# A GRU layer over 128 steps: state weights loaded over 128 rows, and the state kept in the order that this needs

## The chip, the cores and the metric

The kernel runs on one core of one Trainium2 chip. The time is the device time of one execution in microseconds (us). Engines have short names: PE is TensorE (matmuls; PEld its weight loads), ACT is ScalarE, DVE is VectorE, POOL is GpSimd, SP is SyncE, which here only issues DMAs. Each engine works through its own queue in the order of the program.

## The reference, cut to what matters

A GRU layer with a residual, in float32. x is (64 batch rows, 128 steps, 512 features), the state h is (64, 512), first taken from `cond_1024`:

```
for t in 0..127:
    z = sigmoid([x_t, h] @ Wz + bz)
    r = sigmoid([x_t, h] @ Wr + br)
    c = tanh([x_t, r * h] @ Wh + bh)
    h_new = (1 - z) * h + z * c
    out[:, t] = x_t + h_new
    h = tanh(h_new @ Wp + bp) if t % 4 == 3 and t < 127 else h_new
```

Wz, Wr, Wh are (1024, 512): the upper 512 rows multiply x, the lower 512 the state. Wp is (512, 512).

## The kernel before, in words

**Two kinds of matmul.** The products with x do not depend on the state; groups of four steps are computed ahead of time by two levels of a fast (Strassen-like) scheme, as "filler" units that DVE and POOL combine into sums `cp`. The products with the state are the recurrence. Both go through `products` (line 222), a matmul with a 32-column stationary operand.

**Layout.** The 64 batch rows are cut into two halves of 32 (h = 0, 1), the 512 features into four quarters of 128. A state tile is [128 partitions, 2 halves, 128 columns]: partition 32*q + b holds batch row b of a half and quarter q of the features; the 128 columns are the features of the quarter. To multiply, DVE transposes each half in blocks of 32 x 32 (`turn`, line 251). After it, column block k of 32 holds, on partition 32*q + e, the feature that stood in column 32*k + e of quarter q. The rows of a weight tile must lie in the same order: `load_w` (line 96) puts row 128*q + 32*k + e on partition 32*q + e, place k, which takes one DMA of 32 partitions for each quarter. The x side of the kernel has another order already: `load_wx` (line 116) puts row 4p + k on partition p, place k, and `join_x` (line 258) transposes x while reading it with a step of four elements.

**One step of a half** (`half`, line 836): gate r on PE (4 weight blocks x 2), then `crossed` (line 246): two ACTIVATEs of 64 x 128, one for each pair of quarters, from the gate's PSUM bank to r in PSUM; DVE multiplies r * h (line 853) and turns it into rhT (line 854). Meanwhile PE does gate z and some fillers; then the candidate gate from rhT. After both halves' z gates, `gate_z` (line 870) crosses z for both halves, four ACTIVATEs into PSUM, and DVE makes keep = (z - 1) * h (line 873). `crossed` with tanh writes c to SBUF; DVE forms h_new = c * z - keep (lines 912, 925) and turns it into hT for the next step's r gate. In every fourth step the propagation gate (`wp`, `bias_p`) follows, with its own tanh, turn, and fillers. In the last seven steps, z is crossed a half at a time (`late`, line 686). POOL adds h_new to the residual rows `xr` (line 811), and SP stores these four steps at a time.

`seed` (line 395) has ACT copy the sums of the x products into a gate's PSUM bank ahead of its state products, and `copied` (line 513) has ACT take filler sums out of PSUM.

**Order of the work.** The two halves are generators, interleaved by a count of columns with the second 700 behind (lines 951 to 963). `PLACES` (line 623) says how many filler units a half does at three places of a step (between gate z and the candidate gate; after the candidate; after the propagation gate), with one triple for each of the eight steps of a round; the first number is 1 in four of the eight steps and 6 in the other four. `HEAD` gives the first steps more (up to 16), `TAIL` the last ones fewer. A round starts at step 3, 11, 19 and so on.

**The head.** SP and ACT issue the loads of x and of the x weights; `load_wh` (line 149) then loads the state weights gate by gate, two DMAs by SP and two by ACT for each gate; Wp follows by SP alone in `later_loads`. POOL issues the loads of h0 into `h_init`, from which DVE turns the first hT (line 668).

Of the kernel before, what the change touches and what calls it, by code (L numbers as in the profile page):

```python
# [18 lines left out]
def kernel(  # L19
# [14 lines left out]
    nc = tc.nc  # L34
    B, T, D = x.shape
    H = h0.shape[1]
    P = 128
    S = 2
    V = B // S
    NQ = P // V  # L40
    J = H // NQ
    C = 2
    K = D // P
# [28 lines left out]
    wh = [const.tile([P, K, H], F32, name=f"wh_{i}") for i in range(3)]  # L72
    wp = const.tile([P, K, H], F32, name="wp")

    tw_all = const.tile([P, 3, S * NQ * 3 * J // 2], F32, name="tw")
# [6 lines left out]
    gates_in = (Wr, Wz, Wh)  # L82
# [3 lines left out]
    def part(q):  # L86
        return slice(q * V, (q + 1) * V)
# [5 lines left out]
                    out=tile_[part(q), j : j + n, h, :], in_=x[ts(h, V), t0 : t0 + n, ts(q, J)]  # L93
                )

    def load_w(wt, w, k0=0, k1=K, engs=(nc.sync, nc.sync)):
        for q in (0, 2, 1, 3):
            engs[q // 2].dma_start(
                out=wt[part(q), k0:k1, :],
                in_=w[q * P + k0 * V : q * P + k1 * V, :].rearrange("(k e) n -> e k n", e=V),  # L100
            )

    both_queues = (nc.sync, nc.scalar)

    xr = {}
# [10 lines left out]
    def load_wx(i, k0, k1):  # L116
# [2 lines left out]
            in_=gates_in[i][:D].rearrange("(p k) n -> p k n", k=K)[:, k0:k1],  # L119
        )  # L120

    h_init = two.tile([P, S, J], F32, tag="h", name="h_init")
    bias_x = const.tile([P, C, S, 3, J // 2], F32, name="bias_x")
    bias_p = const.tile([P, S, J], F32, name="bias_p")
# [17 lines left out]
    nc.gpsimd.tensor_copy(held, wx[0:1, 2, R, 0:1])  # L142
    for h in range(S):
        nc.gpsimd.dma_start(
            out=h_init[:, h, :],
            in_=h0[ts(h, V), :].rearrange("b (q j) -> q b j", q=NQ),
        )

    def load_wh(i):
        load_w(wh[i], gates_in[i][D:], engs=both_queues)  # L150

    xs = {}

# [23 lines left out]
    def gate_ps(i, h):  # L177
        return rec[2][:, 0] if i == Z else rec[h][:, 0 if i == R else 1]
# [57 lines left out]
    def product(ps, h, lT, w, k, start=False):  # L236
# [6 lines left out]
            start,  # L243
        )

    def crossed(dst, h, i, func):
        for d in range(2):
            nc.scalar.activation(dst[ts(d, 2 * V)], gate_ps(i, h)[ts(h, 2 * V), d, :], func)  # L248

    def turn(dst, src):  # L250
        nc.vector.transpose(out=dst, in_=src)

    def new_T(tag, name):
        return two.tile([P, S, P], F32, tag=tag, name=name)
# [44 lines left out]
    def sum_outer(n):  # L299
        for ka in range(S):  # L300
            if n == 3:
                nc.gpsimd.tensor_sub(tw[3][:, ka], outer(1, 1, ka), outer(0, 1, ka))
            elif n == 2:
                nc.gpsimd.tensor_add(tw[2][:, ka], tw[3][:, ka], outer(0, 0, ka))
            else:
                nc.gpsimd.tensor_sub(tw[4][:, ka], outer(1, 0, ka), tw[2][:, ka])
# [27 lines left out]
    def sum_raw12(g):  # L334
        v = xT[g]
        sx[g, 12] = one.tile([P, 4, C, B], F32, tag="s12r", name=f"s12r_{g}")
        four([sx[g, 12][:, n] for n in range(4)], v[:, 0], v[:, 1])
# [19 lines left out]
    def sum_s34(g):  # L357
        v = xT[g]
        o = sx[g, "o34"] = one.tile([P, 2, 2, P], F32, tag="o34", name=f"o34_{g}")
        nc.gpsimd.tensor_sub(o[:, 0], v[:, 0:2, 0, :], v[:, 2:4, 0, :])  # L360
        nc.gpsimd.tensor_sub(o[:, 1], v[:, 0:2, 1, :], sx[g, "o12"][:, 1])
        s = sx[g, 73] = one.tile([P, 4, 2, B], F32, tag="s73", name=f"s73_{g}")
        four([s[:, n] for n in range(4)], o[:, :, 0], o[:, :, 1])
# [225 lines left out]
    def outer_1(g):  # L589
        with_bias(g, 1, bias0)  # L590

    def outer_c11(g):
        add(c_block(g, 0, 0), m_(g, 1), m_(g, 2))
# [14 lines left out]
    def outer_c22(g):  # L608
        add(c_block(g, 1, 1), m_(g, 7), m_(g, 5))

    def outer_c21(g):
        add(c_block(g, 1, 0), m_(g, 7), m_(g, 4))

    def pair_left(a, p1, p2, g=1):
        with_bias(g, p2, bias0)
        add(c_block(g, a, 0), m_(g, p1), m_(g, p2))

    def pair_right(a, p1, x_, g=1):
        with_bias(g, x_, bias_x[:, 1])
        add(c_block(g, a, 1), m_(g, p1), m_(g, x_))  # L620
# [44 lines left out]
    join_x(0, 2)  # L665
    hT = new_T("hT", "hT_init")
    for h in range(S):
        turn(hT[:, h, :], h_init[:, h, :])
    for i in (1, 2):
        sum_inner(i, nc.vector, slice(2, 3))  # L670
# [86 lines left out]
    def behind_step(t, duo, u, h_new):  # L757
        g, j = divmod(t, Q4)
        even, odd = FIRST + 2 * duo, FIRST + 2 * duo + 1
        if t == T - 7:  # L760
            pair_left(0, 1, 2, LAST)
            pair_right(0, 1, 10, LAST)
        if t == 0:
            sum_outer(2)
            sum_outer(4)
        if t == 3:
            pair_left(1, 8, 9)
            pair_right(1, 8, 11)

        if duo >= 0:  # L770
            if u == 0 and duo >= 1 and odd - 2 < LAST:
                outer_c22(odd - 2)
                outer_c21(odd - 2)
            if even * Q4 < T:
                if u == 0:
                    sum_s34(even)
                elif u == 1:
                    outer_1(even)
                    outer_c11(even)
                    sum_raw12(odd)  # L780
                elif u == 2:
                    outer_u1(even)
                    outer_5(even)
                    sum_raw4(even)
                elif u == 3:
                    outer_c12(even)
                    outer_u2(even)
                    outer_c22(even)
                    if odd < LAST:
                        sum_s12(odd)  # L790
                elif u == 4:
                    if odd < LAST:
                        sum_s34(odd)
                    outer_c21(even)
                    if odd < LAST:
                        outer_1(odd)
                elif u == 5 and odd < LAST:
                    sum_raw4(odd)
                elif u == 6 and odd < LAST:
                    outer_u1(odd)  # L800
                    outer_c11(odd)
                elif u == 7 and odd < LAST:
                    outer_5(odd)
                    outer_c12(odd)
        if duo >= -1 and (even + 2) * Q4 < T:
            if t == 2 or (u == 6 and duo >= 0):
                sum_raw12(even + 2)
            if u == 7:
                sum_s12(even + 2)
        if t < T - 1:  # L810
            nc.gpsimd.tensor_add(xr[g][:, j], xr[g][:, j], h_new)  # L811

        n = 0
        if t >= T - CHUNK:
            n = 3 if t == T - 2 else 0
        elif j == Q4 - 1:
            n = 4
        if n:
            for h in range(S):
                for q in range(NQ):  # L820
                    nc.sync.dma_start(  # L821
                        out=out[ts(h, V), t - n + 1 : t + 1, ts(q, J)],
                        in_=xr[g][part(q), j - n + 1 : j + 1, h, :],
                    )
        if j == 1 and g >= 1 and (g + 1) * Q4 < T:
            new_xr(g + 1)
            load_x(xr[g + 1], (g + 1) * Q4, Q4)
        if t in (1, 2):
            load_xs(t + 2)
        if duo >= 0:  # L830
            if u == 3:
                load_xs(odd + 2)
            elif u == 7:
                load_xs(even + 4)

    def half(h):

        for t in range(T):
            g, j = divmod(t, Q4)
            prop = j == CHUNK - 1 and t < T - 1  # L840
            last = t == T - 1
            duo, u = divmod(t - 3, 8)
# [22 lines left out]
            keep = new_two("keep", t)  # L865
# [4 lines left out]
            def gate_z(part, halves, h_old=h_old, z_=z_, keep=keep):  # L870
                for i in halves:
                    crossed(z_[:, i, :], i, Z, AF.Sigmoid)
                nc.vector.scalar_tensor_tensor(  # L873
                    out=keep[:, part, :],
                    in0=z_[:, part, :],
                    scalar=1.0,
                    in1=h_old[:, part, :],
                    op0=ALU.subtract,
                    op1=ALU.mult,
                )  # L880
                if last:
                    o = xr[g][:, j, part, :]
                    nc.vector.tensor_sub(o, o, keep[:, part, :])

            if h == 1:
                if late(t):
# [19 lines left out]
            h_new = new_two("h", t)  # L906
# [4 lines left out]
            c = z_[:, h, :]  # L911
            nc.vector.tensor_mul(c, cand[:, h, :], c)  # L912
            if last:
                o = xr[g][:, j, h, :]
                nc.vector.tensor_add(o, c, o)
                if h == 0:
                    nc.sync.dma_start(
                        out=out[ts(h, V), t, :].rearrange("b (q n) -> q b n", q=NQ), in_=o
                    )
                else:  # L920
                    for q in (0, 2, 1, 3):
                        both_queues[q // 2].dma_start(out=out[ts(h, V), t, ts(q, J)], in_=o[part(q)])
                return
# [31 lines left out]
    while any(live):  # L955
        h = 0 if live[0] and (not live[1] or at[0] <= at[1]) else 1
# [46 lines left out]
```

## Time and profile before

| | us |
|---|---|
| median of 3 runs | 1260.61 (1259.17 to 1260.79) |
| the profiled execution | 1259.52 |
| its span in the profile | 1257.6 |
| PE busy | 1250.6 (99%) |
| ACT busy | 837.9 (67%) |
| POOL busy | 891.5 (71%) |
| DVE busy | 805.5 (64%) |

A row of the profile names the line, engine and operation, then "out<-in" by the program's names, the shapes, the number of instructions, their busy time and the mean of one in ns, and the engine's idle time before them with what ended it. A row of the timeline has its start and length in us. "PEld" rows are weight loads; here the stationary operand is the turned state, so a PEld row that reads hT or rhT is where PE takes up what DVE has turned.

### The profile page before, as it was taken

How to read it: one execution, taken by the hardware profiler on the slowest of the kernel's cores; microseconds unless marked ns; L12 is line 12 of the kernel's file. 1: busy time of each engine (PE TensorE's matmuls, PEld its weight loads, DVE VectorE, ACT ScalarE, POOL GpSimd, SP SyncE). 2: the span in 40 equal slices, each digit the busy share in tenths (PEclk: the TensorE clock that was granted, in tenths of full speed). 3: DMA queues.
4: the chain of work that ended last, by engine and by line, in shares of the span. 5: the costliest groups of instructions: out<-in, count | busy, mean ns of one | idle time of the engine just before them, and what ended most of it. 6: DMA issues, size and time to landing. Idle time of an engine off the chain costs nothing.

```text
span 1257.6 us, 60730 instructions
## 1 busy us (share of the span) xinstructions
PE 1250.6 (99%) x25960; PEld 1162.1 (92%) x25960; DVE 805.5 (64%) x2173; ACT 837.9 (67%) x2685; POOL 891.5 (71%) x1031
## 2 busy tenths in 40 slices
PE   9999999999999999999999999999999999999998
PEld 4899999999999999999999999999999999999975
DVE  4666666666666666666666666666666666666545
ACT  2566666767666666766666667667676666676665
POOL 3988877776876778767788676786777777677530
PEclk9999999999999999999999999999999999999999
DMA  8311112121121110211211111111111111111010
GB/s 240 91 28 45 49 41 53 36 54 39 34 53 48 41 47 26 53 53 37 53 29 43 53 43 47 38 47 41 53 37 49 40 37 53 42 48 37 9 42 23
DMA packets 113232, 60.82 MB, mean 48 GB/s; under 512 B 12836, under 2 KB 109348, under 8 KB 112964
## 3 DMA queue, kind: packets, MB, share of 16 engines
q1 hardware_dynamic: 111268, 55.00, 16.4%
q8 instruction: 205, 3.36, 1.1%
q10 hardware_dynamic: 1440, 1.80, 0.6%
q14 instruction: 63, 0.52, 0.1%
q0 software_dynamic: 256, 0.14, 0.1%
HBM read 40.11 MB, written 16.78 MB: 45 GB/s over the span
## 4 chain that ended last, share of the span: by engine, by line
PE 98%; DMA 1%; issue 1%; DVE 0%; SPq 0%; POOLq 0%; POOL 0%; ACT 0%; ACTq 0%
PE rec L222 44%; PE rec_z L222 16%; PE scratch_r L222 14%; PE scratch_q L222 11%; PE scratch_a L222 5%; PE scratch_x L222 4%; PE scratch_y L222 4%; DMA wx<-in_L_cond_Wr_dram 0%; SPq L821 0%; DMA xr<-in_x_dram 0%; DMA out_dram<-xr 0%; PE scratch_x L194 0%; DVE z L912 0%; POOLq L998 0%; POOL xr L811 0%
## 5 line engine op out<-in xcount | busy, mean ns | idle before, releaser
L222 PE MATMUL rec<-wh,rhT 128*32 128x256 f32 x4096 | 376.3, 379 | 0.0
L222 PE MATMUL rec<-wh,hT 128*32 128x256 f32 x3072 | 282.6, 379 | 0.0
L222 PE MATMUL rec_z<-wh,hT 128*32 128x256 f32 x3072 | 282.5, 379 | 0.0
L222 PEld LDWEIGHTS rec<-wh,rhT 128*32 128x32 f32 x4096 | 249.6, 110 | 21.1 <-ACT rec L398 1.2
L248 ACT ACTIVATE scratch_r<-rec 64x128 f32<-64x128 f32 x512 | 128.2, 250 | 138.3 <-PE rec L222 63.7
L398 ACT COPY rec<-cp 64x256 f32<-64x256 f32 x512 | 190.6, 372 | 19.9 <-DVE cp L437 0.4
L222 PEld LDWEIGHTS rec<-wh,hT 128*32 128x32 f32 x3072 | 187.4, 110 | 14.7 <-issue 1.8
L222 PEld LDWEIGHTS rec_z<-wh,hT 128*32 128x32 f32 x3072 | 193.8, 110 | 7.2
L248 ACT ACTIVATE rec_z<-rec_z 64x128 f32<-64x128 f32 x488 | 122.2, 250 | 90.1 <-PE rec_z L222 78.6
L248 ACT ACTIVATE c<-rec 64x128 f32<-64x128 f32 x512 | 139.7, 273 | 60.4 <-PE rec L222 48.8
L811 POOL TENSOR_TENSOR xr<-xr,h 128x256 f32<-128x256 f32 x127 | 93.2, 734 | 91.6 <-DVE h L925 91.6
L575 POOL TENSOR_TENSOR mb<-mb,mb 128x768 f32<-128x768 f32 x58 | 106.3, 1833 | 66.8 <-DVE mb L541 66.8
L575 POOL TENSOR_TENSOR cp<-mb,mb 128x768 f32<-128x768 f32 x76 | 139.2, 1831 | 9.5 <-DVE mb L541 5.8
L575 POOL TENSOR_TENSOR cp<-mb 128x768 f32<-128x768 f32 x46 | 84.2, 1831 | 57.0 <-ACT rec_z L398 55.5
L222 PE MATMUL scratch_r<-tw,s 128*32 128x192 f32 x928 | 120.9, 326 | 0.0
L514 ACT COPY cq<-scratch_q 128x384 f32<-128x384 f32 x212 | 102.1, 482 | 19.3 <-PE scratch_q L222 17.8
L531 DVE TENSOR_TENSOR cx<-scratch_r,cx 128x384 f32<-128x384 f32 x106 | 59.1, 558 | 84.1 <-PE scratch_r L222 66.8
L222 PE MATMUL scratch_q<-tt,s 128*32 128x192 f32 x928 | 103.7, 326 | 0.0
L873 DVE SCALAR_TENSOR_TENSOR keep<-rec_z,h 128x256 f32<-128x256 f32 x91 | 38.7, 425 | 95.6 <-ACT rec_z L248 94.6
L537 DVE TENSOR_TENSOR mb<-scratch_q,cx 128x384 f32<-128x384 f32 x106 | 59.1, 558 | 62.4 <-ACT cq L514 62.4
L853 DVE TENSOR_TENSOR rh<-scratch_r,h 128x128 f32<-128x128 f32 x192 | 56.1, 292 | 61.2 <-ACT scratch_r L248 61.2
L222 PE MATMUL rec<-wp,hT 128*32 128x256 f32 x992 | 91.5, 379 | 0.1
(188 smaller groups left out, 3846.5 us busy)
## 6 DMA issues: line engine op xcount, KB each, us to landing
out_dram<-xr SPq DMA_DIRECT2D x249, 64.0 KB, 1.8
xr<-in_x_dram SPq DMA_DIRECT2D x248, 64.0 KB, 2.1
xs<-in_x_dram SPq DMA_DIRECT2D x240, 64.0 KB, 2.0
wx<-in_L_cond_Wr_dram SPq DMA_DIRECT2D x2, 512.0 KB, 5.1
wx<-in_L_cond_Wz_dram SPq DMA_DIRECT2D x1, 1024.0 KB, 5.9
wx<-in_L_cond_Wh_dram SPq DMA_DIRECT2D x1, 1024.0 KB, 8.2
wp<-in_L_cond_Wp_dram SPq DMA_DIRECT2D x4, 256.0 KB, 5.3
wh<-in_L_cond_Wr_dram ACTq DMA_DIRECT2D x2, 256.0 KB, 3.8
```

The costliest lines, as they stand in the source:

```text
L222: nc.tensor.matmul(ps[part(2 * h + c)], lhsT=left, rhs=rhs(c), start=start, stop=True, skip_group_check=True,)
L248: nc.scalar.activation(dst[ts(d, 2 * V)], gate_ps(i, h)[ts(h, 2 * V), d, :], func)
L398: nc.scalar.copy(gate_ps(i, h)[rows].rearrange("p d (c n) -> p d c n", c=C), G[t][rows, :, :, i, :].rearrange("p c d n -> p d c n"),)
L514: nc.scalar.copy(c[:, :nm], ps[:, :nm])
L531: nc.vector.tensor_add(T2[what][:, :nm], r_ps[:, :nm], T2[what][:, :nm])
L537: nc.vector.tensor_add(blocks(1, 1), runs(q_ps[:, :nm]), runs(T2[what][:, :nm]))
L575: nc.gpsimd.tensor_add(dst, a, b)
L811: nc.gpsimd.tensor_add(xr[g][:, j], xr[g][:, j], h_new)
L853: nc.vector.tensor_mul(rh[:, h, :], r_, h_old[:, h, :])
L873: nc.vector.scalar_tensor_tensor(out=keep[:, part, :], in0=z_[:, part, :], scalar=1.0, in1=h_old[:, part, :], op0=ALU.subtract, op1=ALU.mult,)
```

## The change

- `load_w` makes two DMAs of all 128 partitions, each with two neighbouring rows per partition: row 4p + k of the weight goes to partition p, place k. SP issues all of them; ACT issues no weight loads any more.
- So that the turned state has the same order, the state's columns are kept as column 32*k + e for feature 4*e + k of the quarter. `crossed` reads the gate's bank as it lies and writes each element to its place: four neighbouring features go to four places 32 elements apart. This holds for r, z, c and the propagated state.
- h0 is loaded into a part of the `tw` tile that is not yet in use (`h_rows`), and two ACT copies bring it into the state's order in `h_init`.
- POOL's residual add goes over the row of `xr` in steps of four elements, with h_new read as it lies. The last step's two DVE operations for each half do the same.

The count of matmuls, their shapes and their order on PE are the same.

```diff
-    def load_w(wt, w, k0=0, k1=K, engs=(nc.sync, nc.sync)):
-        for q in (0, 2, 1, 3):
-            engs[q // 2].dma_start(
-                out=wt[part(q), k0:k1, :],
-                in_=w[q * P + k0 * V : q * P + k1 * V, :].rearrange("(k e) n -> e k n", e=V),
+    def load_w(wt, w):
+        for k0 in (0, 2):
+            nc.sync.dma_start(
+                out=wt[:, k0 : k0 + 2, :],
+                in_=w.rearrange("(p k) n -> p k n", k=K)[:, k0 : k0 + 2],
             )
...
+    h_rows = tw_all[:, 2, : S * J].rearrange("p (h u) -> p h u", h=S)
...
-            out=h_init[:, h, :],
+            out=h_rows[:, h, :],
...
     def load_wh(i):
-        load_w(wh[i], gates_in[i][D:], engs=both_queues)
+        load_w(wh[i], gates_in[i][D:])
...
+    def plain_order(v):
+        return v.rearrange("p (e k) -> p e k", k=K)
+
+    def state_order(v):
+        return v.rearrange("p (k e) -> p e k", k=K)
+
     def crossed(dst, h, i, func):
         for d in range(2):
-            nc.scalar.activation(dst[ts(d, 2 * V)], gate_ps(i, h)[ts(h, 2 * V), d, :], func)
+            nc.scalar.activation(
+                state_order(dst[ts(d, 2 * V)]),
+                plain_order(gate_ps(i, h)[ts(h, 2 * V), d, :]),
+                func,
+            )
...
     for h in range(S):
+        nc.scalar.copy(state_order(h_init[:, h, :]), plain_order(h_rows[:, h, :]))
         turn(hT[:, h, :], h_init[:, h, :])
...
-            nc.gpsimd.tensor_add(xr[g][:, j], xr[g][:, j], h_new)
+            o = xr[g][:, j].rearrange("p h (e k) -> p h k e", k=K)
+            nc.gpsimd.tensor_add(o, o, h_new.rearrange("p h (k e) -> p h k e", k=K))
...
-                    o = xr[g][:, j, part, :]
-                    nc.vector.tensor_sub(o, o, keep[:, part, :])
+                    o = plain_order(xr[g][:, j, part, :])
+                    nc.vector.tensor_sub(o, o, state_order(keep[:, part, :]))
...
-                nc.vector.tensor_add(o, c, o)
+                nc.vector.tensor_add(plain_order(o), state_order(c), plain_order(o))
```

More of the change, by code (lines that the diff above doesn't have):

```diff
@@ L810, in behind_step @@
         if t < T - 1:
-            nc.gpsimd.tensor_add(xr[g][:, j], xr[g][:, j], h_new)
+            o = xr[g][:, j].rearrange("p h (e k) -> p h e k", k=K)
+            nc.gpsimd.tensor_add(o, o, h_new.rearrange("p h (k e) -> p h e k", k=K))
         n = 0
```

## The prediction, made blind

> **What bounds the kernel now.** I read the page first (busy shares, then the chain that ended last), then the costliest groups, then the timeline of one eight-step round, engine by engine.
>
> ```profile
> span 1257.6 us, 60730 instructions
> PE 1250.6 (99%) x25960; PEld 1162.1 (92%) x25960; DVE 805.5 (64%) x2173; ACT 837.9 (67%) x2685; POOL 891.5 (71%) x1031
> ...
> PE 98%; DMA 1%; issue 1%; DVE 0%; SPq 0%; POOLq 0%; POOL 0%; ACT 0%; ACTq 0%
> ...
> L248 ACT ACTIVATE scratch_r<-rec 64x128 f32<-64x128 f32 x512 | 128.2, 250 | 138.3 <-PE rec L222 63.7
> ...
> L248 ACT ACTIVATE rec_z<-rec_z 64x128 f32<-64x128 f32 x488 | 122.2, 250 | 90.1 <-PE rec_z L222 78.6
> L248 ACT ACTIVATE c<-rec 64x128 f32<-64x128 f32 x512 | 139.7, 273 | 60.4 <-PE rec L222 48.8
> L811 POOL TENSOR_TENSOR xr<-xr,h 128x256 f32<-128x256 f32 x127 | 93.2, 734 | 91.6 <-DVE h L925 91.6
> ```
>
> TensorE (PE) carries 98% of the chain and is busy for 99% of the span; the gate ACTIVATEs of line 248, which the change touches, appear in that chain with 0%. That says only that today they come just in time. Whether they stay in time is read from a round of the recurrence: when does a turned state or r*h leave VectorE, and when does PE load it?
>
> One step has a single filler between its z and its candidate gate (the tight kind). ScalarE, VectorE and weight loads of its end:
>
> ```profile
> 656.84 1.10 ACT L248 ACTIVATE rec_z<-rec_z 64x128 f32<-64x128 f32 x4 [0.79 <-PE rec_z L222]
> 657.96 0.55 ACT L248 ACTIVATE c<-rec 64x128 f32<-64x128 f32 x2
> 658.55 0.37 ACT L398 COPY rec<-cp 64x256 f32<-64x256 f32 x1
> 658.94 0.56 ACT L248 ACTIVATE c<-rec 64x128 f32<-64x128 f32 x2
> ...
> 659.27 0.31 DVE L251 STREAM_TRANSPOSE hT<-h 128x128 f32<-128x128 f32 x1
> ...
> 659.75 0.14 PEld L222 LDWEIGHTS rec<-wh,hT 128*32 128x32 f32 x2
> ```
>
> Columns are start, length, instruction. ScalarE has no gap here: four sigmoids of z, then at once the two tanh of the first half, a seed copy, the two tanh of the second half. The first half's hT ends at 659.58 and PE loads it at 659.75, 0.17 later. PE is full because its queue is cut to fit ScalarE, with tenths of a microsecond to spare.
>
> **The change, part by part.**
>
> Strided writes. Every crossing (r, z, tanh, and the propagation's tanh) writes with a step of 32 elements instead of 1: 512 + 512 + 488 in the rows above, and the few late z and the propagation's beside them; no instruction is added to the steps. What one such write costs no row shows. The floor is nothing, since all ACTIVATEs of the trace write runs. The nearest rows are of another engine, a stepped read:
>
> ```profile
> L264 DVE STREAM_TRANSPOSE xT<-xs 128x256 f32<-128x256 f32 x120 | 74.3, 639 | 2.2 <-DMA out_dram<-xr 0.4
> ...
> L853 DVE TENSOR_TENSOR rh<-scratch_r,h 128x128 f32<-128x128 f32 x192 | 56.1, 292 | 61.2 <-ACT scratch_r L248 61.2
> L873 DVE SCALAR_TENSOR_TENSOR keep<-rec_z,h 128x256 f32<-128x256 f32 x91 | 38.7, 425 | 95.6 <-ACT rec_z L248 94.6 <-PE rec L222 1.0
> ...
> L251 DVE STREAM_TRANSPOSE hT<-h 128x128 f32<-128x128 f32 x254 | 79.2, 312 | 8.7
> ...
> L514 ACT COPY cq<-scratch_q 128x384 f32<-128x384 f32 x212 | 102.1, 482 | 19.3 <-PE scratch_q L222 17.8
> ```
>
> Packed VectorE work goes from 292 to 425 ns for 128 more columns, 1.04 ns each. A packed transpose of 128 columns takes 312, so one of 256 should take 445; line 264 reads with a step of four elements and takes 639: 194 ns more, 0.76 ns per element. (If transposes cost 82 ns per block of 32, 312 to 639 needs no step penalty; that is the other reading.) ScalarE itself takes (482 - 273) / 256 = 0.82 ns per packed element, so one extra beat per element would be 105 ns, and the VectorE price 97 ns. I take e = 0.10 us per ACTIVATE; ends: 0 and 0.20 (two extra beats).
>
> The Trainium skill bears on this choice. "SBUF — State Buffer", section "Door 1: The DMA port swizzle", says that memory lines are 16 bytes, that two hits per line are needed for full speed, and that fp32 can step by four for free; a step of 32 elements then pays at each element. By that rule the sum is the one below. "ScalarE: Activation LUTs", section "Step-by-step: what each stage is for", gives one element per cycle and lane whatever the function, 0.833 ns, without a word on steps; by that alone e is 0 and the sum is 1261 us. The trace agrees with the latter for packed writes (0.82 ns) and shows no stepped one.
>
> What e does to a tight step. In the step above, z takes 4e = 0.4 longer, so the tanh behind it starts 0.4 later and takes 2e = 0.2 longer: hT ends at 659.58 + 0.60, and PE, which needs at least 0.11 from a turn's end to its load (605.62 to 605.73 below), loads at 660.29 instead of 659.75: **0.54 us** of PE lost. PE is in order, so the other half's work behind it waits too. Two more steps of the round are worse, since their r*h has no slack either:
>
> ```profile
> 606.55 1.09 ACT L248 ACTIVATE rec_z<-rec_z 64x128 f32<-64x128 f32 x4 [0.17 <-PE rec_z L222]
> 607.72 0.56 ACT L248 ACTIVATE c<-rec 64x128 f32<-64x128 f32 x2
> ...
> 618.14 1.09 ACT L248 ACTIVATE rec_z<-rec_z 64x128 f32<-64x128 f32 x4 [0.48 <-PE rec_z L222]
> 619.26 0.55 ACT L248 ACTIVATE c<-rec 64x128 f32<-64x128 f32 x2
> ...
> 605.31 0.31 DVE L251 STREAM_TRANSPOSE rhT<-rh 128x128 f32<-128x128 f32 x1
> ...
> 609.04 0.31 DVE L251 STREAM_TRANSPOSE hT<-h 128x128 f32<-128x128 f32 x1
> ...
> 620.51 0.31 DVE L251 STREAM_TRANSPOSE hT<-h 128x128 f32<-128x128 f32 x1
> ...
> 605.73 0.14 PEld L222 LDWEIGHTS rec<-wh,rhT 128*32 128x32 f32 x3
> ...
> 609.60 0.14 PEld L222 LDWEIGHTS rec<-wp,hT 128*32 128x32 f32 x2
> ...
> 621.06 0.14 PEld L222 LDWEIGHTS rec<-wh,hT 128*32 128x32 f32 x2
> ```
>
> In the step around 605, r's two ACTIVATEs make rhT 0.2 late and PE stalls 0.2 at once; z starts 0.2 later, takes 0.4 longer and ends at 608.24 instead of 607.64, which moves the tanh from 607.72 to 608.26, by 0.54, and hT by 0.74: 609.35 + 0.74 + 0.11 = 610.20 against 609.60, **0.60** in all. In the step around 619 the tanh follows z directly (618.14 + 1.09, then 619.26), so nothing of the 0.2 + 0.4 is absorbed: 620.82 + 0.80 + 0.11 = 621.73 against 621.06: **0.67**. The remaining kinds of step:
>
> ```profile
> 647.82 0.31 DVE L251 STREAM_TRANSPOSE hT<-h 128x128 f32<-128x128 f32 x1
> ...
> 648.62 0.14 PEld L222 LDWEIGHTS rec<-wp,hT 128*32 128x32 f32 x2
> ...
> 678.25 0.31 DVE L251 STREAM_TRANSPOSE hT<-h 128x128 f32<-128x128 f32 x1
> ...
> 678.68 0.14 PEld L222 LDWEIGHTS rec<-wh,hT 128*32 128x32 f32 x2
> ...
> 629.96 0.31 DVE L251 STREAM_TRANSPOSE hT<-h 128x128 f32<-128x128 f32 x1
> ...
> 630.79 0.14 PEld L222 LDWEIGHTS rec<-wh,hT 128*32 128x32 f32 x2
> ```
>
> Tight with 0.49 to spare: 648.13 + 0.60 + 0.11 - 648.62 = **0.22**. The last step of a round, six fillers before its candidate gate so that z is long done: only 2e, 678.56 + 0.20 + 0.11 - 678.68 = **0.19**. The three loose steps (630.27 + 0.31 against 630.79): **0**. That is 2.22 us a round for the first half. The second half's tanh follows the seed copy at once (658.94 after 658.92), so its turn is 8e late; I add 0.09 for it in each of the five steps: 2.67 us a round. The first seven steps have up to 16 fillers and lose nothing; the other 121 are 15 rounds: **40 us**. What is late next is ScalarE's copies of filler sums, which queue behind the crossings; I charge nothing, as PE's own stall gives them the same time.
>
> POOL's residual add (734 ns) now reads and writes xr with a step of four. Between 0 and double, 0 to 93 us of POOL over 127 adds; POOL is idle for 1257.6 - 891.5 = 366 us, 91.6 of them just before these adds, waiting for h. Nearest is the transposes' 0.76 ns on 256 elements, 0.2 each. Charged: 0, cover as named.
>
> Loads and head. Twelve issues for the three gate weights (six on ScalarE's queue, six on SP's) become six, all on SP; the propagation's go from four to two. Transfers are half as many and twice as large.
>
> ```profile
> 17.36 2.09 ACTq L98 DMA_DIRECT2D wh<-in_L_cond_Wh_dram  x2
> 25.56 0.53 ACT L248 ACTIVATE scratch_r<-rec 64x128 f32<-64x128 f32 x2 [7.98 <-DMA wh<-in_L_cond_Wh_dram]
> ...
> 30.68 0.33 PEld L222 LDWEIGHTS rec<-wh,rhT 128*32 128x32 f32 x4
> ...
> 19.43 1.55 SPq L98 DMA_DIRECT2D wh<-in_L_cond_Wh_dram  x2
> ...
> wh<-in_L_cond_Wh_dram SPq DMA_DIRECT2D x2, 256.0 KB, 8.9
> ```
>
> The last weight is issued by 20.98 and lands 8.9 later, near 29.5, for a use at 30.68; PE does not wait for it, so an earlier landing buys nothing, and a landing up to 1 us later costs nothing. SP has as many gate-weight issues as before, so the x loads queued behind them are not pushed back. The two ACT copies that reorder h0 (0.4 us each by line 398's row) stand in ScalarE's 7.98 us of idleness before 25.56; hT is needed only after them. The end gets four stepped VectorE operations, 0.1 each by the transposes' price, two in series: 0.2.
>
> Sum: 1259.5 us (the profiled execution, 1257.6 of it the span) + 40 + 0.2 = 1299.7; the median of the runs, 1260.6, stands 1.1 higher, so about **1300 us**.
>
> **The rivals.**
>
> 1. The stepped write is free. Speaking for it: the second reading of line 264, and that no row of the trace shows a stepped write paying. Then every PE slack above stays, head and end give +0.2, and the time is 1261 (1258.5 to 1263).
> 2. Half the price, or only where one of PSUM (r, z) and SBUF (tanh) is dear, e near 0.05: the working above gives 0.20 + 0.27 + 0.24 + 0 + 0.09 for the same five steps (0.24 is the first one's), with the second half about 0.85 a round: 13 us, 1274 (1264 to 1285).
> 3. Dearer, e = 0.20: the slacks are used up once, the rest grows in proportion, 1.40 + 1.47 + 1.14 + 0.82 + 0.39 and 0.2 each for the second half, 6.2 us a round: 93 us, 1354 (1320 to 1360).
> 4. Faster: the weights, in 128-row pieces and without ScalarE's issues, land earlier and let the head close up. It would need PE to wait for them in the head; the price would be 3 us if the first gates started that much earlier. Against it: their landing is ahead of use, as shown. It decides from 2.5 us on: 1257.
>
> **How the numbers follow.** 0.2%, about what a measurement of this kernel can tell from no change, is 2.5 us. Full price 0.42 (its own range 1285 to 1320), half price 0.12, dearer 0.08: slower 0.62. Free writes 0.31: same. Head 0.07: faster. The forecast is the full price, 1300; the range reaches down to the free case at 1259 and up to 1320, leaving out the dearer case and the faster one.
>
> **What would show it.** Right: line 248's means rise from 250 and 273 to near 350 and 373; ScalarE's busy time from 838 by 0.1 for each of the 1512 and more, to about 1000; the idle time before weight loads of rhT and hT grows, mostly after z in tight steps; the first step's load at 659.75 moves behind its turn by the same 0.11 as at 605.73, and a round grows by 2.67 us. Wrong: line 248 unchanged means rival 1. The add of line 811 shows POOL's price by itself. If means rise but the round does not, PE's slack was larger than the turns' ends say; if the round grows much more than 2.67, the copies behind the crossings hold PE's banks.

## The result, and the profile after

The kernel after takes 1279.5 us (median of four runs, 1279.11 to 1279.97) against 1260.05 us for the kernel before (1259.17 to 1260.79): a ratio of 1.0151 (95% interval 1.0135 to 1.0167), 19.4 us more. The forecast was 1300, within 1259 to 1320: the sign was right, the amount twice too large.

Two corrections to the description above. The last step's two VectorE operations of each half do not go over `xr` in steps of four, as POOL's add does: they walk `xr` as it lies and read the other operand (`keep`, then z * c) with a step of 32 elements (`plain_order` and `state_order`). And z is crossed a half at a time in six of the last seven steps, not in all of them: `late` leaves out step T - 6.

The page of the kernel after: span, busy times, the shares of the chain that ended last, and five groups (here `crossed` is line 255, the residual add line 824, the turn line 262).

```profile
span 1277.1 us, 60721 instructions
PE 1266.3 (99%) x25960; PEld 1145.7 (90%) x25960; DVE 812.3 (64%) x2173; ACT 922.5 (72%) x2687; POOL 909.9 (71%) x1031
...
PE 96%; ACT 2%; issue 1%; DMA 1%; DVE 1%; SPq 0%; POOLq 0%; POOL 0%; ACTq 0%; DVEq 0%
...
L255 ACT ACTIVATE c<-rec 64x128 f32<-64x128 f32 x512 | 206.4, 403 | 48.6 <-PE rec L223 39.7
L255 ACT ACTIVATE scratch_r<-rec 64x128 f32<-64x128 f32 x512 | 128.0, 250 | 124.2 <-DVE mb L551 68.1
L824 POOL TENSOR_TENSOR xr<-xr,h 128x256 f32<-128x256 f32 x127 | 111.0, 874 | 99.0 <-DVE h L938 99.0
L255 ACT ACTIVATE rec_z<-rec_z 64x128 f32<-64x128 f32 x488 | 122.0, 250 | 79.5 <-PE rec_z L223 68.0
...
L925 DVE TENSOR_TENSOR rec_z<-c,rec_z 128x128 f32<-128x128 f32 x244 | 72.2, 296 | 62.6 <-ACT c L255 62.3
```

Read the means. r (out scratch_r) and z (out rec_z) write with the new step and take 250 ns, exactly as before: both write to PSUM. The tanh c writes to SBUF and went from 273 to 403 ns. The same split shows where the shapes are kept apart (the view of groups by form of the kernel after): the propagation's tanh and the late z (24 crossings in six of the last seven steps) also write to SBUF, and both pay. The last three rows are the two h0 copies and the stepped operations at the end.

```profile
L255 ACT ACTIVATE hprop<-rec 64x128 f32<-64x128 f32 x124 | 50.1, 404 | 9.1 <-PE rec L223 7.6
L255 ACT ACTIVATE z<-rec_z 64x128 f32<-64x128 f32 x24 | 9.4, 393 | 2.4 <-PE rec_z L223 2.1
L679 ACT COPY h_init<-tw 128x128 f32<-128x128 f32 x2 | 0.7, 433 | 0.0
L896 DVE TENSOR_TENSOR xr<-xr,keep 128x128 f32<-128x128 f32 x2 | 0.8, 378 | 0.1
L928 DVE TENSOR_TENSOR xr<-z,xr 128x128 f32<-128x128 f32 x2 | 0.7, 372 | 0.1
```

The tight step that the prediction worked through (z at 656.84 before), in the timeline of the kernel after; columns are start, length, instruction:

```profile
664.08 1.09 ACT L255 ACTIVATE rec_z<-rec_z 64x128 f32<-64x128 f32 x4 [0.77 <-PE rec_z L223]
665.20 0.82 ACT L255 ACTIVATE c<-rec 64x128 f32<-64x128 f32 x2
666.05 0.37 ACT L409 COPY rec<-cp 64x256 f32<-64x256 f32 x1
666.45 0.81 ACT L255 ACTIVATE c<-rec 64x128 f32<-64x128 f32 x2
...
666.78 0.31 DVE L262 STREAM_TRANSPOSE hT<-h 128x128 f32<-128x128 f32 x1
...
667.21 0.14 PEld L223 LDWEIGHTS rec<-wh,hT 128*32 128x32 f32 x3 [0.19 <-issue]
```

The four sigmoids still take 1.09. The two tanh of the first half take 0.82 instead of 0.55, so hT ends 0.27 later behind z than before. PE now loads it 0.12 after its end (667.09 to 667.21) instead of 0.17: the spare time is gone, and PE waits.

One round of eight steps, from a load of hT in the last step of a round to the same load a round later, in the view of windows. First the kernel before, then the kernel after; columns are window, length, busy us of PE, PEld, DVE, ACT and POOL (instructions), granted clock, DMA share, GB/s.

```profile
601.80:678.68 76.88, 76.88 (x1624) 73.62 (x1617) 50.41 (x136) 52.77 (x170) 56.69 (x67) 1.00 0.16 43
```

```profile
608.43:686.28 77.85, 77.85 (x1619) 71.85 (x1616) 50.84 (x135) 57.87 (x170) 57.90 (x67) 1.00 0.16 43
```

This round is 0.97 us longer with the same matmuls, but for a few at the edges of the windows, at the same clock. PE is "busy" for all of both windows: a matmul's record (0.38 us) overlaps its followers, so a stall of a tenth or two does not open a gap in it. The loss shows only in the round's length and in the weight loads, whose busy time falls from 73.62 to 71.85 us.

Where the 19.4 us come from, by the start of PE's work on each r gate in the two traces: up to step 6 the kernel after falls 0.55 us behind; then 14 rounds cost 0.94 each (13.1 us; 13.6 behind at step 116); the last twelve steps bring it to 18.6 (the second half's r gate) and the end to 19.4, the difference of the spans. The tail thus loses more per step than the rounds do. There the late z also goes to SBUF (393 ns where it was 273).

The head gained nothing. SP issues all weight loads now, but the first weight load for h is at 23.17 us instead of 23.34, and within six steps that lead has turned into the 0.55 of lag.

### The profile page after: what moved, and what is told of

It is laid out like the page before. It is cut to its first block, busy times and chain, and to the rows that moved or that the text cites. A ratio compares the mean times of both kernels' runs of the same rounds, so it can differ in the third digit from the quotient of the medians.

```text
span 1277.1 us, 60721 instructions
## 1 busy us (share of the span) xinstructions
PE 1266.3 (99%) x25960; PEld 1145.7 (90%) x25960; DVE 812.3 (64%) x2173; ACT 922.5 (72%) x2687; POOL 909.9 (71%) x1031
## 4 chain that ended last, share of the span: by engine, by line
PE 96%; ACT 2%; issue 1%; DMA 1%; DVE 1%; SPq 0%; POOLq 0%; POOL 0%; ACTq 0%; DVEq 0%
PE rec L223 43%; PE rec_z L223 16%; PE scratch_r L223 11%; PE scratch_q L223 10%; PE scratch_a L223 5%; PE scratch_x L223 5%; PE scratch_y L223 5%; ACT c L255 1%; DMA wx<-in_L_cond_Wr_dram 0%; ACT z L255 0%; DMA out_dram<-xr 0%; ACT rec L409 0%; DVE h L938 0%; ACT scratch_r L255 0%; SPq L834 0%
## 5 line engine op out<-in xcount | busy, mean ns | idle before, releaser
L223 PE MATMUL rec<-wh,rhT 128*32 128x256 f32 x4096 | 393.5, 379 | 0.0
L223 PE MATMUL rec<-wh,hT 128*32 128x256 f32 x3072 | 300.7, 380 | 1.5 <-DVE hT L262 1.1
L223 PE MATMUL rec_z<-wh,hT 128*32 128x256 f32 x3072 | 300.0, 379 | 0.0
L223 PEld LDWEIGHTS rec<-wh,rhT 128*32 128x32 f32 x4096 | 253.6, 110 | 19.9 <-ACT scratch_r L255 2.5
L255 ACT ACTIVATE c<-rec 64x128 f32<-64x128 f32 x512 | 206.4, 403 | 48.6 <-PE rec L223 39.7
L223 PEld LDWEIGHTS rec_z<-wh,hT 128*32 128x32 f32 x3072 | 199.6, 110 | 7.9
L824 POOL TENSOR_TENSOR xr<-xr,h 128x256 f32<-128x256 f32 x127 | 111.0, 874 | 99.0 <-DVE h L938 99.0
L925 DVE TENSOR_TENSOR rec_z<-c,rec_z 128x128 f32<-128x128 f32 x244 | 72.2, 296 | 62.6 <-ACT c L255 62.3
L223 PE MATMUL rec<-wp,hT 128*32 128x256 f32 x992 | 96.8, 379 | 0.9 <-DVE hT L262 0.5
L223 PE MATMUL rec<-wh,hpT 128*32 128x256 f32 x992 | 94.1, 379 | 0.0
```

The lines of the kernel that those rows point to most:

```text
L223: nc.tensor.matmul(ps[part(2 * h + c)], lhsT=left, rhs=rhs(c), start=start, stop=True, skip_group_check=True,)
L255: nc.scalar.activation(state_order(dst[ts(d, 2 * V)]), plain_order(gate_ps(i, h)[ts(h, 2 * V), d, :]), func,)
L824: nc.gpsimd.tensor_add(o, o, h_new.rearrange("p h (k e) -> p h e k", k=K))
```

## The experiments

The theory: only writes that go to SBUF pay for the step, the tanh of the steps above all, and each tanh pair delays its turn beyond PE's small reserve. Against it stood the dearer residual add on POOL (734 to 874 ns), the loads, and an effect of the sigmoids that their means hide.

**One part alone, one part undone.** `e1_tanh_plain` undoes the tanh's step:

```diff
-                state_order(dst[ts(d, 2 * V)]),
+                (state_order if func is AF.Sigmoid else plain_order)(dst[ts(d, 2 * V)]),
```

> The changed kernel, but tanh (the candidate c and the propagated state) writes its columns as they lie, while r and z still write with a step; c therefore meets the state in the wrong order and the output is not the reference's. Theory A (the price is that of a stepped ScalarE write into SBUF, 403 instead of 273 ns, and the tanh carry it): tanh back at 273 ns, time 1260 to 1263 us, the rest above 1260 from the 24 late z that still go to SBUF with a step. Theory B (POOL's residual add, 874 instead of 734 ns, delays the filler sums): at least 1270 us. Theory C (the loads, the head): at least 1270 us.

`e2_tanh_stepped_only` is the kernel before with the step in the tanh alone:

```diff
+            o = dst[ts(d, 2 * V)].rearrange("p (e k) -> p e k", k=K)
+            if func is AF.Tanh:
+                o = dst[ts(d, 2 * V)].rearrange("p (k e) -> p e k", k=K)
...
+                o,
+                gate_ps(i, h)[ts(h, 2 * V), d, :].rearrange("p (e k) -> p e k", k=K),
```

> The kernel before, with one part of the change alone: tanh writes with a step of 32 elements (c and the propagated state come out in another order than the rest, so the output is not the reference's). Theory A: 1276 to 1279 us, line 248's tanh at 403 ns. Theory B or C: 1260 to 1265 us.

`e3_pool_plain` gives POOL its plain add back:

```diff
-            o = xr[g][:, j].rearrange("p h (e k) -> p h e k", k=K)
-            nc.gpsimd.tensor_add(o, o, h_new.rearrange("p h (k e) -> p h e k", k=K))
+            nc.gpsimd.tensor_add(xr[g][:, j], xr[g][:, j], h_new)
```

> The changed kernel, with POOL's residual add unstepped as before (it adds the state's columns in their own order, so the residual is not the reference's). Theory A: the add is back at 734 ns and the time stays, 1278.5 to 1280 us, since POOL idles before the add. Theory B: 1260 to 1272 us.

`e4_loads_only` is the kernel before with the new loads alone:

```diff
+    def load_w(wt, w):
+        for k0 in (0, 2):
+            nc.sync.dma_start(
+                out=wt[:, k0 : k0 + 2, :],
...
+        load_w(wh[i], gates_in[i][D:])
```

> The kernel before, with the new load_w alone (128-row loads, all by SP; the weights' rows then lie in another order than the state's, so the output is not the reference's). Theory A: 1259.5 to 1260.5 us, PE's first state gate within 0.2 us of before. Theory C: several us off, up or down.

Measured, all beside the same runs of the kernel before (1259.76 us):

| | us | ratio to before (95%) |
|---|---|---|
| tanh plain again (e1) | 1262.32 | 1.0019 (1.0010 to 1.0028) |
| only tanh stepped (e2) | 1277.10 | 1.0133 (1.0118 to 1.0148) |
| POOL's add plain (e3) | 1279.68 | 1.0156 (1.0141 to 1.0171) |
| only the loads (e4) | 1259.48 | 0.9995 (0.9986 to 1.0005) |

The two means that belong to this, tanh in e1 and then the residual add in e3, from the views of groups:

```profile
L255 ACT ACTIVATE c<-rec 64x128 f32<-64x128 f32 x512 | 138.9, 271 | 60.0 <-PE rec L223 48.4
```

```profile
L823 POOL TENSOR_TENSOR xr<-xr,h 128x256 f32<-128x256 f32 x127 | 93.0, 733 | 104.9 <-DVE h L937 104.9
```

The tanh's step alone gives 17.3 us of loss, and without it 2.6 are left; together that is the whole 19.4 within the intervals. In e1's trace the rounds are as long as before; its last r gate starts 1.9 late, 0.45 of it from the head and 1.4 from the tail, where late z still writes to SBUF with the step, and the rest of the 2.6 comes after that (its span is 2.5 longer). POOL's add, back at 733 ns, brings nothing: its extra 0.14 us had indeed been covered. The loads change nothing by themselves.

**The price by itself.** `e5_probe` adds rows of six equal instructions behind the last step, so its total time has them in it; only the rows count.

```diff
+    for n in range(6):
+        nc.scalar.activation(step(big, 4), src_ps, AF.Tanh)
...
+    for n in range(6):
+        nc.scalar.activation(turned(big), src_ps, AF.Tanh)
...
+    for n in range(6):
+        nc.scalar.activation(turned(flat_ps), src_ps, AF.Tanh)
```

> The kernel before, with rows of six instructions each put behind the last step: ScalarE writes of 64x128 from PSUM into SBUF with steps of 1, 2, 3, 4 and 32 elements, in the change's order, and in pairs; the same into PSUM with steps 1, 4 and the change's order; a stepped ScalarE read; VectorE and POOL adds with one stepped operand. Theory A (the destination decides): tanh and sigmoid in the change's order into SBUF both near 400 ns against 273, into PSUM 250 at every step. Rival A' (the function decides: tanh pays, sigmoid does not): sigmoid into SBUF stays at 273, tanh into PSUM rises. Open: from which step on SBUF writes pay; by the VectorE row that was used in the prediction, 4 elements already pay.

The probe's rows, views of groups by form in the window behind the last step, sorted here by line. Lines 984 to 998 are ACT from PSUM to SBUF (tt): writes with a step of 1, 2, 3, 4 and 32, the change's order with tanh, pairs of neighbours 8 apart, the change's order with sigmoid. Lines 1000 and 1004 write to PSUM, as a run and in the change's order. Lines 1006 and 1008 read SBUF, in the change's order and as a run. Lines 1012 to 1016 are VectorE on SBUF: runs, one input stepped, the output stepped. Lines 1018 to 1024 are POOL: runs, one input with a step of four (as the change's add reads `xr`), one input with a step of 32, the output with a step of 32.

```profile
L984 ACT ACTIVATE tt<-rec 64x128 f32<-64x128 f32 x6 | 1.6, 271 | 1.7 <-DVE xr L915 1.6
...
L986 ACT ACTIVATE tt<-rec 64x128 f32<-64x128 f32 x6 | 1.7, 278 | 0.2
...
L988 ACT ACTIVATE tt<-rec 64x128 f32<-64x128 f32 x6 | 2.0, 333 | 0.2
...
L990 ACT ACTIVATE tt<-rec 64x128 f32<-64x128 f32 x6 | 2.3, 388 | 0.2
...
L992 ACT ACTIVATE tt<-rec 64x128 f32<-64x128 f32 x6 | 2.3, 378 | 0.2
...
L994 ACT ACTIVATE tt<-rec 64x128 f32<-64x128 f32 x6 | 2.3, 380 | 0.2
...
L996 ACT ACTIVATE tt<-rec 64x128 f32<-64x128 f32 x6 | 1.7, 279 | 0.2
...
L998 ACT ACTIVATE tt<-rec 64x128 f32<-64x128 f32 x6 | 2.3, 380 | 0.2
...
L1000 ACT ACTIVATE rec<-rec 64x128 f32<-64x128 f32 x6 | 1.5, 247 | 0.2
...
L1004 ACT ACTIVATE rec<-rec 64x128 f32<-64x128 f32 x6 | 1.5, 247 | 0.2
...
L1006 ACT ACTIVATE tt<-wx 64x128 f32<-64x128 f32 x6 | 2.5, 421 | 0.2
L1008 ACT ACTIVATE tt<-wx 64x128 f32<-64x128 f32 x6 | 1.9, 309 | 0.2
...
L1012 DVE TENSOR_TENSOR tt<-wx 128x128 f32<-128x128 f32 x6 | 1.8, 292 | 0.2
...
L1014 DVE TENSOR_TENSOR tt<-wx 128x128 f32<-128x128 f32 x6 | 2.2, 372 | 0.2
...
L1016 DVE TENSOR_TENSOR tt<-wx 128x128 f32<-128x128 f32 x6 | 2.3, 376 | 0.2
...
L1018 POOL TENSOR_TENSOR tt<-wx 128x256 f32<-128x256 f32 x6 | 3.7, 611 | 43.6 <-DVE tt L1016 43.2
...
L1020 POOL TENSOR_TENSOR tt<-wx 128x256 f32<-128x256 f32 x6 | 5.1, 842 | 0.5
L1022 POOL TENSOR_TENSOR tt<-wx 128x256 f32<-128x256 f32 x6 | 4.9, 822 | 0.5
L1024 POOL TENSOR_TENSOR tt<-wx 128x256 f32<-128x256 f32 x6 | 3.8, 628 | 0.5
```

The function does not matter (380 for sigmoid and tanh), the memory does: 247 ns into PSUM in either order, 271 to 388 into SBUF (near 400 had been expected for the change's order, which takes 380 here). Nor does the length of the jump count, but how many elements lie close together: pairs cost 279, a step of two 278, of three 333, of four and more 378 to 388. The Trainium skill, "SBUF — State Buffer", section "Door 1: The DMA port swizzle", states that a memory line has 16 bytes and that two hits per line are needed for full speed. The rows agree as to the pairs and the step of two, each of which puts two fp32 values into a line. The same passage lets fp32 step by four for free, and there the measurement decides: 388 against 271.

**Does the price follow the memory in the kernel?** `e6_all_into_sbuf` moves r and z to SBUF, so that all crossings should pay:

```diff
-    r_ = scratch[r_bank][:, 3 * J :]
+    r_ = const.tile([P, J], F32, name="r_sb")
+    z_sb = const.tile([P, S, J], F32, name="z_sb")
...
-            z_ = z
+            z_ = z_sb
```

> The changed kernel with r and z of every step moved from PSUM to SBUF, so that all its crossings pay (the output is the reference's). This tests the working of the prediction with the price that it assumed everywhere. By theory A r and z rise from 250 to about 403 ns, and the prediction's sums with 0.153 for r and z and 0.13 for tanh give 0.81 + 0.98 + 1.05 + 0.49 + 0.25 a round and at least 0.09 each for the second half, 4.0 to 4.3 us a round, 1320 to 1328 us with the tail. If PE's slack were larger than the turns' ends say (rival), below 1305 us.

Measured: 1503.31 us, ratio 1.1929 (1.1913 to 1.1946), far above what was expected. The groups of e6 show why:

```profile
L256 ACT ACTIVATE r_sb<-rec 64x128 f32<-64x128 f32 x512 | 206.0, 402 | 243.6 <-PE rec L224 181.4 <-DVE rh L867 55.8 <-PE rec_z L224 1.5
L256 ACT ACTIVATE z_sb<-rec_z 64x128 f32<-64x128 f32 x488 | 195.7, 401 | 37.8 <-PE rec_z L224 32.7
L939 DVE TENSOR_TENSOR h<-z_sb,keep 128x128 f32<-128x128 f32 x244 | 181.5, 744 | 15.4 <-DVE z_sb L926 0.9
L867 DVE TENSOR_TENSOR rh<-r_sb,h 128x128 f32<-128x128 f32 x192 | 144.7, 754 | 114.4 <-ACT r_sb L256 112.8
```

The sigmoids' 402 and 401 ns are as the theory has them. But r * h and h_new, which took 292 with one operand in PSUM, now average 754 and 744, and that is another cause. The timeline of e6, VectorE first, then POOL at the same place:

```profile
704.92 0.29 DVE L939 TENSOR_TENSOR h<-z_sb,keep 128x128 f32<-128x128 f32 x1
...
707.67 1.77 DVE L867 TENSOR_TENSOR rh<-r_sb,h 128x128 f32<-128x128 f32 x1 [0.29 <-ACT r_sb L256]
```

```profile
705.29 0.87 POOL L825 TENSOR_TENSOR xr<-xr,h 128x256 f32<-128x256 f32 x1 [1.52 <-DVE h L939]
707.47 1.83 POOL L592 TENSOR_TENSOR mb<-mb,bias_d 128x768 f32<-128x768 f32 x1 [1.31 <-DVE mb L553]
```

While POOL is idle, VectorE takes 0.29. The product that begins at 707.67, under a POOL instruction, ends at 709.44, just after that one (709.30). Of the 510 products r * h and differences h_new of e6, all with both inputs in SBUF, 278 take over 400 ns. Every one of these began under a POOL instruction and ended 0.14 to 0.16 us behind the end of one. Of the 232 short ones 188 began while POOL was idle, 40 under a POOL instruction with 0.25 us or less to go, and four ran in 0.29 although the POOL instruction had 0.6 us or more to go. So e6 confirms the price of a stepped write to SBUF for r and z, but its time says nothing on the arithmetic of slack. That needed another experiment (e10).

**The step elsewhere.** Three versions keep the rest of the change and move c's step away from ACT's write. `e7_c_walked_in_psum` writes c as a run, and the product c * z walks z and its output, both in PSUM:

```diff
+                (plain_order if i == H_ else state_order)(dst[ts(d, 2 * V)]),
...
+            nc.vector.tensor_mul(state_order(c), plain_order(cand[:, h, :]), state_order(c))
```

> The changed kernel, but ScalarE writes c into SBUF as it lies; VectorE's product c * z runs in that order and steps through z and its own result in PSUM instead (output as the reference). Theory A and no price for VectorE's steps in PSUM: product near 294 ns, time 1261 to 1263 us (the propagated state and the late z still step in SBUF). If VectorE pays there as in SBUF (0.09 us): 1263 to 1267 us.

`e8_c_read_stepped` has the product read c from SBUF with a step of four:

```diff
+                c.rearrange("p (k e) -> p k e", k=K),
+                cand[:, h, :].rearrange("p (e k) -> p k e", k=K),
+                c.rearrange("p (k e) -> p k e", k=K),
```

> The changed kernel, but ScalarE writes c as it lies and VectorE reads c from SBUF with a step of four elements (output as the reference). By the last step's rows (378 instead of 292 ns with a stepped operand) the product takes 380 ns, on the path once a half instead of twice 0.13: 0.1 to 0.25 us a round, 1263 to 1267 us. If a step of four elements is free for a read: 1261 to 1263 us.

`e9_read_stepped` turns all crossings round: ACT reads the gate's bank in PSUM with a step of four and writes runs.

```diff
-                state_order(dst[ts(d, 2 * V)]),
-                plain_order(gate_ps(i, h)[ts(h, 2 * V), d, :]),
+                dst[ts(d, 2 * V)].rearrange("p (k e) -> p k e", k=K),
+                gate_ps(i, h)[ts(h, 2 * V), d, :].rearrange("p (e k) -> p k e", k=K),
```

> The changed kernel with the step moved from the write to the read: the crossings go through the gate's PSUM bank in steps of four elements and write every destination packed (the h0 copies too; the output is the reference's). Theory A, and PSUM reads free of a step's price as PSUM writes are: r and z near 250 ns, tanh near 272, a round as before, 1259.5 to 1261.5 us; the loads alone gave 1259.48, so no gain over the kernel before beyond 0.1%. If a stepped PSUM read pays about 0.1 us: all crossings pay, 1295 us or more.

The deciding row of each, in this order (product, product, tanh), from the views of groups:

```profile
L925 DVE TENSOR_TENSOR rec_z<-c,rec_z 128x128 f32<-128x128 f32 x244 | 71.8, 294 | 17.5 <-ACT c L255 13.2
```

```profile
L925 DVE TENSOR_TENSOR rec_z<-c,rec_z 128x128 f32<-128x128 f32 x244 | 96.6, 396 | 14.6 <-ACT c L255 10.2
```

```profile
L255 ACT ACTIVATE c<-rec 64x128 f32<-64x128 f32 x512 | 138.9, 271 | 61.0 <-PE rec L223 49.4
```

| | us | ratio to before (95%) | loss in a round |
|---|---|---|---|
| step in PSUM, by VectorE (e7) | 1265.08 | 1.0038 (1.0025 to 1.0051) | 0.15 |
| step in SBUF, by VectorE (e8) | 1267.20 | 1.0054 (1.0038 to 1.0069) | about 0.28 |
| step in PSUM, read by ACT (e9) | 1260.20 | 1.0004 (0.9995 to 1.0013) | 0 |

The kernel before took 1260.52 us beside e7 and e8, 1259.70 beside e9 and e10. VectorE too walks PSUM for nothing (294 ns, a run takes 296 or less) and pays 100 ns in SBUF. What e7 left stepped in SBUF are the propagation's tanh (404 ns) and the tail's late z, whose product there takes 398; its rounds lose 0.15, and the larger half of its 4.6 us lies in the tail. So e7 missed its expectation: 1261 to 1263 us had been expected if VectorE's steps in PSUM were free, and they are, but the two stepped writes that it kept cost more than was thought. e8, 0.2 above its range, keeps them too. e9 has all of the change (the loads, the state's order, POOL's add at 872 ns) and the time of the kernel before: only the side on which the step lies made the 19.4 us. It is 1.5% faster than the kernel after; no version here beats the kernel before.

**The arithmetic of slack.** `e10_bias_operand` is the kernel before with a column of zeros as bias operand in every crossing, which lengthens r, z and tanh alike, as the prediction had assumed of the step:

```diff
+    nought = const.tile([P, 1], F32, name="nought")
+    nc.gpsimd.memset(nought, 0.0)
...
+                bias=nought[ts(h, 2 * V)],
```

> The kernel before, with a column of zeros as the bias operand of every crossing: each ACTIVATE of r, z and tanh gets longer by some amount e while all destinations and VectorE's operands stay (output as the reference). It tests the prediction's working with a price that is really the same everywhere: by its sums 0.85 us a round for e = 0.05 and 2.67 for e = 0.10, so 1274 us for the one and 1300 for the other, and in between in proportion to the e that line 248's rows show. Rival (PE's slack is larger than the turns' ends say): less than half of that.

Groups of e10, then one round of it in the view of windows:

```profile
L250 ACT ACTIVATE c<-rec,nought 64x128 f32<-64x128 f32 x512 | 186.0, 363 | 39.4 <-PE rec L224 31.2
...
L250 ACT ACTIVATE rec_z<-rec_z,nought 64x128 f32<-64x128 f32 x488 | 161.5, 331 | 47.0 <-PE rec_z L224 34.2
```

```profile
626.50:705.11 78.61, 78.52 (x1624) 70.21 (x1618) 50.64 (x135) 61.47 (x170) 56.70 (x67) 1.00 0.17 43
```

Measured: 1290.82 us, ratio 1.0247 (1.0231 to 1.0262). r and z went up by 81 ns, tanh by 90. Two forecasts can be held against this. The prediction's sums for the first half, with these prices in place of its 0.10, give 0.44 + 0.47 + 0.54 + 0.12 + 0.17 = 1.74 us a round; the round grew by 78.61 - 76.88 = 1.73. Its two totals, 1274 for 0.05 and 1300 for 0.10, give about 1292 at 0.084, against 1290.82 measured. So the rival is out, and a price that is the same everywhere costs about what the working says.

That holds for the sum and not for its parts. With the second half's share the totals stand for about 2.1 us a round, more than the 1.77 that the rounds lost on average; the head (1.3 us behind at step 6) and the last twelve steps with the end (5.8) make up the difference, which is luck. And step by step, by the start of PE's z gate in the first half, the five steps of the sums lose 0.30, 0.54, 0.33, 0.28 and 0.15, and one loose step, for which the sums have nothing, 0.19. The working was right in total for a uniform price. The price of the change was not uniform.

## Why the prediction was right in sign and twice too large

**What bounds the kernel now: right.** PE carried the chain with tenths of a microsecond to spare. In the kernel after the turn is taken up 0.12 after its end, as close as the 0.11 that the prediction allowed.

**The step that failed: "Strided writes", "I take e = 0.10 us per ACTIVATE"**, for every crossing. It was one price for all destinations, drawn from a VectorE row that reads SBUF. Measured: 0 for r and z, which write to PSUM (250 and 250 ns), and 0.13 for the tanh, which writes to SBUF (273 to 403). The tanh was undersized by a quarter, but r and z were the larger part of the sum: in the tight step, z's 4e was 0.4 of the 0.60 us that hT was to come later. The prediction's own description names the two destinations, and its second rival speaks of "only where one of PSUM (r, z) and SBUF (tanh) is dear". That is what happened. It was put at 0.12 and priced as an even 0.05 for all crossings (1274), where it should have been worked out with e in the tanh alone.

**The five slacks: near in total once the price is right, with one crossing left out.** With 0.26 for a tanh pair and nothing for r and z, the same sums are 659.58 + 0.26 + 0.11 - 659.75 = 0.20 for the first step, 609.35 + 0.37 - 609.60 = 0.12, 620.82 + 0.37 - 621.06 = 0.13, below nothing for the step around 647, and 678.56 + 0.37 - 678.68 = 0.25 for the last: 0.70 us a round. Measured were 0.94. By the start of PE's z gate in the first half, averaged over 13 rounds, the two steps that end in a propagation (around 605 and 647) lose 0.25 and 0.19, where the sums have 0.12 and nothing. The other three lose 0.10, 0.15 and 0.25, a little less than their sums. What the sums leave out is the propagation's own tanh, whose turn PE loads for the next r gate: the prediction names it among the crossings and gives it no term, and it went from 273 to 404 ns. In e7 it is the only stepped write to SBUF within the rounds, and they lose 0.15, all of it in the two steps that end in a propagation. About 0.1 us a round is left. It may be the second half's tanh, for which the prediction charged 0.09 in each of five steps; no run separates that.

**The ends were mis-sized.** The prediction let the first seven steps lose nothing. In them the kernel after goes from 0.17 us ahead to 0.55 behind, and e2, which has the tanh's step alone, from 0.12 ahead to 0.62 behind, so this is the tanh. The prediction counted the last steps like a round's, and overlooked that late z goes to SBUF. The last twelve steps and the end cost 5.8 us (19.4 - 13.6), where a round's rate gives 1.4. Two runs separate this: e2, with no late z stepped, loses 3.1 there (13.7 behind at step 116, 16.7 at the end), and e1, with late z and the end stepped but no tanh, loses 2.1 (0.45 and 2.5). That is 5.2 of the 5.8; the rest is open. The stepped VectorE operations at the end cost what was said: 378 and 372 ns, against 292 for the first of them before.

**POOL: right that it is covered.** The add took 0.14 more (0.2 by the prediction's nearest row), and giving it back did not move the time. **Loads and head: right.** The loads alone are worth nothing (0.9995), SP's queue delayed nothing, and the two h0 copies (433 ns, forecast 0.4) lie in ACT's idle time. The last state weight, put near 29.5 (20.98 + 8.9 would be 29.9), landed at 29.15 before, so its margin was as good as said. The rival "faster" falls with them; "the stepped write is free" is true of PSUM alone, and "dearer" holds for no destination.

**What would show it.** Line 248's means were to be near 350 and 373 and the round 2.67 us longer; they are 250 and 403, and 0.94. ACT's busy time was to reach about 1000 us and is 922.5: the 660 SBUF writes (512 + 124 + 24) of 0.12 to 0.13 more each make up its rise of 84.6.

## What to carry to other kernels

In these runs a stepped fp32 access had no price of its own: the price belonged to the memory and the engine that touched it. So look at each destination before one number is given to a whole class of instructions. Where data crosses from PSUM to SBUF and must be reordered on the way, put the step on the PSUM side (here read by ScalarE, at no cost), and the run on the SBUF side. Where a busy engine has tenths of a microsecond in reserve, read that reserve from a producer's end to the consumer's first instruction and sum it by kind of step; the busy share showed 99% before and after.

## What the runs showed of the hardware that was not expected

- ScalarE's write of 128 fp32 elements per lane to SBUF costs 271 ns as a run, 278 with a step of two, 279 as pairs, 333 with a step of three and 378 to 388 from four on. To PSUM it costs 247 in either order. A stepped read from SBUF costs too (309 to 421), one from PSUM does not (e9).
- POOL's add of 256 columns pays for a stepped read (611 ns as runs, 842 with a step of four, 822 with one of 32) and hardly for a stepped write (628).
- In e6 a VectorE product or difference with both fp32 inputs in SBUF that began under a POOL instruction ended, but for four of 322, only behind the end of that one: r * h took between 283 and 1947 ns in e6, where one PSUM operand had kept it at 292. The Trainium skill, "GPSIMD Engine Reference", section "Specifications", says that the two engines share their SBUF interfaces and that VectorE instructions with two SBUF inputs contend. The traces agree. I put most of the 224 us that e6 takes more than the kernel after down to it: the expectation with the dearer sigmoids alone was 1328 at most. That is an estimate, as no run has the one without the other.
